# The last batch's second layer: seven products of eighths inside each of seven quarter products

## The chip, the cores and the metric

One core of a Trainium2 chip runs the whole program. The metric is the device time of one execution in microseconds. The core's engines have a queue each and run their own instructions in order: TensorE (PE; its weight loads are listed as PEld), VectorE (DVE), ScalarE (ACT), GpSimd (POOL) and SyncE (SP), which in this kernel issues all DMAs. TensorE writes only into PSUM banks; VectorE or ScalarE must read a bank before it is written anew.

## What is computed

The input x is [4, 2048, 512], f32. Two sublayers follow each other, each with a layer norm in front, a layer norm on its result, and a residual sum:

```python
x = x + _layernorm(_L0_attn_ref(_layernorm(x), w_qkv))       # windowed attention, 16 heads
x = x + _layernorm(_L0_ffn_ref(_layernorm(x), gate..., W1, b1, W2, b2, TW1, Tb1, TW2, Tb2))
```

The second one mixes its weights for each batch b from a base and eight experts, with gates g that are means over the batch's tokens:

```python
mW1 = W1 + jnp.einsum('be,efh->bfh', g, TW1)     # [2048, 512] for each b
mW2 = W2 + jnp.einsum('be,ehf->bhf', g, TW2)     # [512, 2048] for each b
u   = gelu(x @ mW1.T + mb1)                      # first layer
out = u @ mW2.T + mb2                            # second layer
```

## The kernel before, in words

**Stages.** The first half of the time is attention, the second the feed-forward part (from about 1660 us). Under both, a generator, `mixer` (L103), mixes the weights: each step issues the load of an expert's chunk three steps ahead (`load`, L118) and one VectorE instruction (L144). After eight experts of a chunk come four VectorE sums of its quarters (L152 to L155), and one step later the stores to DRAM (`store`, L121 to L132). The steps are written out by hand into the order of the other work: `next(blend)` in attention, `mixing(...)` with a count for each place in the feed-forward part. The DMAs of a step stand in SyncE's queue where the step stands.

**Blocks.** The feed-forward part goes over 16 blocks K of 512 tokens, four to a batch. A block has a first layer of four sets (`begin`, `middle`, `end`), then a second layer (`second`, L1065 on), then the next block follows without a break. `end` of a set (its last product and three pairs of gelus) is put into the next set, and that of the last set into the second layer's first product (`closing`).

**Seven products.** Both layers are done by Winograd's form of Strassen's algorithm: a product of 2x2 quarters by seven products of quarters and sums of quarters. In the second layer a quarter product takes 256 tokens, 1024 hidden units and 256 outputs: `product2` (L1049) runs over 8 chunks of 128 hidden units and 2 token tiles, the tokens' side as the weights of 128x128 and the mixed weights (w2s) as 256 moving columns. Every f32 matmul call leaves two records in the trace. The seven left factors, A11, A12, S1, S2, S4, S3 and A22, lie in DRAM (`m2_d`), 1 MB each; `load_second` (L1042) loads them three products ahead, into three buffers. The right factors are quarters of u and sums of them: t1 and t3 are made by GpSimd in `more_sums` (L1033, L1034); t1 is updated by four GpSimd instructions of 128x512 after product 1 (L1093), and the quarter b21 by four more after product 2 (L1099), each chunk as soon as TensorE has read it. VectorE adds each bank into the block's result y (L1075), and at the end takes the row statistics (`stats`, L87 and L89, GpSimd for the root, L91 and L93). ScalarE normalizes (`standard`, L1165) and VectorE adds the residual (`finish`, L1170), for all blocks but the last one within the next block's sets.

**The next block.** `load_block` (L301) loads the next block's input, fxT, after the second layer's product 0; `right_sums` (L311 to L314) makes four sums over it on VectorE after product 2.

**The last block** does product 6 in two halves by token tile (L1125 on), so that the first tile's rest goes beside the second tile's matmuls; the statistics of a row tile are joined from two halves (`summed`).

**Pools.** The `mix` pool has "exps" (4 buffers), "acc" (2) and "sums" (1). PSUM has eight banks: x and z twice and y once for the first layer, x2, z2 and y2 for the second.

Of the kernel before, what the change touches and what calls it, by code (L numbers as in the profile page):

```python
# [9 lines left out]
F32 = mybir.dt.float32  # L10
# [24 lines left out]
def sandwich(ctx: ExitStack, tc: tile.TileContext, x, w_qkv, gw1, gb1, gw2, gb2, w1, b1, w2, b2, tw1, tb1, tw2, tb2, out):  # L35
# [43 lines left out]
    }  # L79
    m2_d = {b: dram.tile([P, 7, HC, Q], F32, name=f"m2d_{b}") for b in range(NB)}  # L80
    mb2_d = {b: dram.tile([P, D], F32, name=f"mb2d_{b}") for b in range(NB)}
    A11, A12, S1, S2, S4, S3, A22 = range(7)

    def stats(src, tag):
# [16 lines left out]
    def mixer():  # L101
# [19 lines left out]
        def store(b, s, c, acc, sums):  # L121
            rows = acc.rearrange("p h (q d) -> p h q d", d=Q)
            if s == 0:
                early, later = (m1_d[b, c - c % 2, i][:, c % 2] for i in range(2))
                nc.sync.dma_start(early[:, A11 : A12 + 1, :], rows[:, 0])
                nc.sync.dma_start(early[:, S1 : S2 + 1, :], sums[:, 0:2, :])
                nc.sync.dma_start(later[:, S4 - 4, :], sums[:, 2, :])
                nc.sync.dma_start(later[:, S3 - 4 : A22 - 3, :], rows[:, 1])
            else:
                nc.sync.dma_start(m2_d[b][:, A11 : A12 + 1, c, :], rows[:, :, 0, :])  # L130
                nc.sync.dma_start(m2_d[b][:, S1 : S4 + 1, c, :], sums)
                nc.sync.dma_start(m2_d[b][:, S3 : A22 + 1, c, :], rows[:, :, 1, :])  # L132
# [4 lines left out]
        for n, (b, s, c, e) in enumerate(todo):  # L137
# [8 lines left out]
            if e == NX - 1:  # L146
# [9 lines left out]
                late.append(lambda b=b, s=s, c=c, acc=acc, sums=sums: store(b, s, c, acc, sums))  # L156
                yield
        for f in late:
            f()
# [147 lines left out]
    def right_sums(K):  # L307

        b11, b12, b21, b22 = quarters(K)
        t = tT_of[K] = wp.tile([P, 4, 2, Q], F32, tag="w1", name=f"tT_{K}")  # L310
        nc.vector.tensor_tensor(t[:, 0], b12, b11, ALU.subtract)  # L311
        nc.vector.tensor_tensor(t[:, 2], b22, b12, ALU.subtract)
        nc.vector.tensor_tensor(t[:, 1], b22, t[:, 0], ALU.subtract)
        nc.vector.tensor_tensor(t[:, 3], b21, t[:, 1], ALU.subtract)  # L314

# [5 lines left out]
    def hidden(cc, K, pool):  # L321

        if cc in (0, HC):
            t = wp.tile([P, 3, 2, Q], F32, tag="s1" if cc == 0 else "s2", name=f"u{cc}_{K}")
            return t[:, :2].rearrange("p f h t -> p f (h t)")
        return pool.tile([P, 2, TB], F32, tag=f"u{cc}", name=f"u{cc}_{K}")

    us = {}
    blend = mixer()


    with ExitStack() as actx:
# [469 lines left out]
        first[244].append(lambda: load_first(0, 2, 1, wp, "tx"))  # L802
        rest[243].append(lambda: right_sums(0))

# [133 lines left out]
    with ExitStack() as fctx:  # L938
# [90 lines left out]
        def more_sums(K, c):  # L1029

            b12, b22 = us[c][:, :, Q:], us[c + HC][:, :, Q:]
            t1s[c] = wts.tile([P, 2, Q], F32, tag=f"t1_{c}", name=f"t1_{c}_{K}")
            nc.gpsimd.tensor_tensor(t1s[c], b12, us[c][:, :, :Q], ALU.subtract)  # L1033
            nc.gpsimd.tensor_tensor(b12, b22, b12, ALU.subtract)  # L1034
            b, k = divmod(K, NBLK)
            if k == NBLK - 1 and b + 1 < NB:
                for i in range(2):
                    load_first(b + 1, c, i, *home(c, i))

        order = [A11, S1, A12, S2, S4, S3, A22]  # L1040

        def load_second(g):  # L1042

            K, j = divmod(g, 7)
            if K < NBK:
                w2s[g] = wts.tile([P, HC, Q], F32, tag="w2s", bufs=3, name=f"w2s_{g}")
                nc.sync.dma_start(w2s[g], m2_d[K // NBLK][:, order[j]])

        def product2(K, j, bank, right, start, closing=None, tiles=range(2)):  # L1049

            w = w2s[7 * K + j]
            for c in range(HC):
                if c == 2 and closing:
                    end(*closing)
                for t in tiles:
                    nc.tensor.matmul(  # L1056
                        bank[:, t, :],
                        lhsT=right(c - c % 2)[:, c % 2, ts(t, P)],
                        rhs=w[:, c, :],
                        start=(start and c == 0 and t == tiles[0]),  # L1060
                        stop=True,
                        skip_group_check=True,
                    )
            load_second(7 * K + j + 3)

# [3 lines left out]
        def second(K, closing, steps, load_x1):  # L1069
# [47 lines left out]
            Y = bank2("y2", f"py2b_{K}")  # L1117
            if K + 1 < NBK:
                product2(K, 6, Y, b21, True)
                for t in range(2):  # L1120
                    pending.append((K, t + 2, y[1][:, t, :], stats(y[1][:, t, :], f"d{K}_{t + 2}")))
                add(c21, Y, c21)
                steps()
                for t in range(2):
                    pending.append((K, t, y[0][:, t, :], stats(y[0][:, t, :], f"d{K}_{t}")))  # L1125
                yield
                return

            Z = bank2("z2", f"pz2b_{K}")
            product2(K, 6, Y, b21, True, tiles=(0,))  # L1130
            product2(K, 6, Z, b21, True, tiles=(1,))
            for t in range(2):
                standard(K, t + 2, y[1][:, t, :], stats(y[1][:, t, :], f"d{K}_{t + 2}"))
            halves = [small.tile([P, 2, 6], F32, tag="halves", bufs=2, name=f"halves_{t}") for t in range(2)]
            for t in range(2):
                nc.vector.bn_stats(halves[t][:, 0, :], c11[:, t])
            def summed(t, bank):
                nc.vector.tensor_tensor(c21[:, t], bank[:, t, :], c21[:, t], ALU.add)
                nc.vector.bn_stats(halves[t][:, 1, :], c21[:, t])
                mv = small.tile([P, 2], F32, tag="mv", name=f"mv_e{t}")  # L1140
                nc.vector.bn_aggr(mv, halves[t])
                rs = small.tile([P, 1], F32, tag="rs", name=f"rs_e{t}")
                nc.gpsimd.tensor_scalar(rs, mv[:, 1:2], EPS, None, ALU.add)
                nc.gpsimd.tensor_tensor(rs, rs, mhalf, ALU.pow)
                return mv, rs

            sm = summed(0, Y)
            for t in range(2):
                finish(K, t + 2, y[1][:, t, :])
            normalize(y[0][:, 0, :], y[0][:, 0, :], sm)  # L1150
            sm = summed(1, Z)
            finish(K, 0, y[0][:, 0, :])
            normalize(y[0][:, 1, :], y[0][:, 1, :], sm)
            finish(K, 1, y[0][:, 1, :])
            yield

# [66 lines left out]
        nc.sync.dma_start(win[last]["x"], x[NB - 1, L - P :])  # L1223
        for g in range(3):
            load_second(g)
        pending, normed_y = [], []
# [11 lines left out]
        for K in range(NBK):  # L1238
# [5 lines left out]
            for c in range(0, HC, 2):  # L1244
# [32 lines left out]
                for f in hooks.get(("set", n), ()):  # L1277
                    f()
            for j, _ in enumerate(second(K, before, mixing(3, 2, 3, 2, 2, 3, 2), load_x1)):

                if j == (0 if K else 3) and K + 1 < NBK:
                    load_block(K + 1)
                if j == (2 if K else 5) and K + 1 < NBK:
                    right_sums(K + 1)
                for f in hooks.get(("product", K, j), ()):
# [57 lines left out]
```

## Time and profile before

| | |
|---|---|
| median of three runs | 3230.07 us (3229.55 to 3233.14) |
| span of the profiled execution | 3228.7 us |
| TensorE busy | 3211.8 us, 23190 matmul records |
| granted TensorE clock, mean | 0.999 |
| second layer, all 16 blocks (L1056) | 32 records a product, 379 ns each as a record, 6.91 us a product in the chain |
| mixing, VectorE (L144) | 512 instructions of 1361 ns |
| VectorE busy in 2886 to 2934 us (a second layer of the last batch) | 11.57 of 48 us |
| VectorE busy in 2838 to 2886 us (a first layer of the last batch) | 7.93 of 48 us |
| DMA share and rate in 2700 to 2740 us (mixing) | 1.04, 400 GB/s |
| DMA share and rate in 2886 to 2934 us | 0.49, 169 GB/s |

The page gives no other time for the profiled execution than its span; the median of the runs is 1.4 us above it. A record's mean (379 ns) is its time from start to end; records overlap, so the spacing of a stream is the length of a merged stretch by the number of its records. The timeline merges equal instructions that follow each other: start, length, engine, line, operation, output and inputs by name, count, and in brackets the idle time in front and what ended it. The mixing of the last chunk ends at 2778 us; the last batch's blocks (12 to 15) begin at 2835, 2932, 3028 and 3125 us.

### The profile page before, as it was taken

To read this page: it belongs to the slowest core of one execution; us is meant where nothing else is said; L and a number is where in the kernel's file an instruction comes from. 1 tells how busy PE (TensorE), PEld (TensorE's weight loads), DVE (VectorE), ACT (ScalarE), POOL (GpSimd) and SP (SyncE) were. 2 spreads that over 40 slices of the span, in tenths; PEclk is the share of its full clock that TensorE was granted. 3 is DMA by queue.
4 is the path that set the end of the run, shared out by engine and by line. 5 is a ranking of instruction groups with operands and counts; after the bars stand their busy time and mean duration, and the time that the engine had idled before them with its cause. 6 is when DMAs were issued, how large, how long until landed. Compare 5 with 4: busy or idle time off the path is not lost.

```text
span 3228.7 us, 59302 instructions
## 1 busy us (share of the span) xinstructions
PE 3211.8 (99%) x23190; PEld 2690.1 (83%) x23190; DVE 2142.8 (66%) x2995; ACT 1566.3 (49%) x4288; POOL 660.1 (20%) x843
## 2 busy tenths in 40 slices
PE   9999999999999999999999999999999999999999
PEld 7788878788787887878768888888888888888888
DVE  5766666888998889888865665777656776222212
ACT  3777777777777777777761222111222111222111
POOL 0111111111111111110112332333332333231222
PEclk9999999999999999999999999999999999999999
DMA  2111112455555556554687889998889988622332
GB/s 87 50 60 54 41 59 81 131 187 169 196 193 166 177 177 201 192 177 151 220 283 272 317 310 344 352 341 329 318 320 348 355 330 327 238 98 90 131 111 98
DMA packets 316121, 652.02 MB, mean 202 GB/s; under 512 B 22969, under 2 KB 89657, under 8 KB 295490
## 3 DMA queue, kind: packets, MB, share of 16 engines
q1 hardware_dynamic: 315842, 648.22, 57.3%
q8 instruction: 184, 3.01, 0.4%
q14 instruction: 95, 0.78, 0.1%
HBM read 538.03 MB, written 110.10 MB: 201 GB/s over the span
## 4 chain that ended last, share of the span: by engine, by line
PE 96%; DMA 2%; DVE 1%; ACT 1%; issue 0%; POOL 0%; SPq 0%; POOLq 0%; DVEq 0%; ACTq 0%
PE pm L453 23%; PE px L958 13%; PE ptp L621 11%; PE px L1056 10%; PE sc L584 7%; PE pz L958 7%; PE pz L1056 6%; PE po L642 5%; PE py L958 3%; PE py L1056 3%; PE py2b L1056 3%; DMA exps<-in_tw 1%; PE pm L517 1%; PE ptx L287 1%; PE pto L258 1%; PE pt_a L382 1%
## 5 line engine op out<-in xcount | busy, mean ns | idle before, releaser
L144 DVE SCALAR_TENSOR_TENSOR acc<-exps,g,acc 128x1024 f32<-128x1024 f32 x512 | 697.0, 1361 | 75.0 <-DMA exps<-in_tw 69.0
L593 DVE TENSOR_REDUCE nm<-sc 128x2 f32<-128x768 f32 (+1 forms) x512 | 449.3, 918 | 207.7 <-PE sc L584 202.6
L606 ACT ACTIVATE pr<-sc,nm 128x384 f32<-128x384 f32 (+1 forms) x1024 | 572.8, 592 | 10.0 <-DVE nm L593 9.8
L626 ACT COPY prT<-ptp 128x512 f32<-128x512 f32 x732 | 382.9, 595 | 281.4 <-PE ptp L621 281.1
L995 ACT COPY py<-px 128x512 f32<-128x512 f32 x63 | 36.0, 571 | 784.3 <-PE px L958 784.2
L621 PEld LDWEIGHTS ptp<-ident,pr 128*128 128x128 f32 x2944 | 318.1, 141 | 102.3 <-issue 89.8
L621 PE MATMUL ptp<-ident,pr 128*128 128x128 f32 x2944 | 378.9, 278 | 0.0
L958 PE MATMUL px<-tT,w 128*128 128x256 f32 x1512 | 349.6, 379 | 0.6 <-DVE cpv L1018 0.6
L958 PEld LDWEIGHTS px<-tT,w 128*128 128x128 f32 x1512 | 287.2, 190 | 40.0 <-DVE cpv L1018 1.0
L584 PE MATMUL sc<-k,q 32*128 32x384 f32 (+2 forms) x2816 | 243.0, 423 | 3.5 <-ACT pr L606 3.3
L606 ACT ACTIVATION_READ_ACCUMULATOR pr<-sc,nm 128x1 f32 x1024 | 236.5, 231 | 0.0
L1015 DVE TENSOR_TENSOR cpb<-pz,cpb 128x512 f32<-128x512 f32 x63 | 43.4, 690 | 284.7 <-PE pz L958 247.5
L1056 PE MATMUL px<-w2s,u 128*128 128x256 f32 x1024 | 228.9, 379 | 0.7 <-ACT last L292 0.7
L1056 PEld LDWEIGHTS px<-w2s,u 128*128 128x128 f32 x1024 | 194.5, 190 | 27.3 <-ACT last L292 0.9
L91 POOL TENSOR_SCALAR ve_b<-mv_b 128x1 f32<-128x1 f32 x64 | 42.8, 669 | 818.1 <-DVE mv_b L89 818.1
L642 PEld LDWEIGHTS po<-prT,v 128*32 128x32 f32 x5888 | 152.2, 110 | 50.9 <-ACT pr L606 25.4
L642 PE MATMUL po<-prT,v 128*32 128x128 f32 x5888 | 189.7, 275 | 0.2
L584 PEld LDWEIGHTS sc<-k,q 32*128 32x128 f32 x2816 | 118.4, 183 | 74.3 <-issue 53.9
L1033 POOL TENSOR_TENSOR t<-u 128x512 f32<-128x512 f32 x64 | 83.5, 1304 | 464.2 <-ACT u L970 452.2
L453 PE MATMUL pm<-xnT,wqkv 128*128 128x256 f32 x720 | 172.2, 382 | 0.0
L1075 DVE TENSOR_TENSOR y<-px,mb 128x512 f32<-128x512 f32 x48 | 33.1, 690 | 195.8 <-PE px L1056 195.8
L453 PEld LDWEIGHTS pm<-xnT,wqkv 128*128 128x128 f32 x720 | 132.0, 190 | 16.7
(231 smaller groups left out, 5602.2 us busy)
## 6 DMA issues: line engine op xcount, KB each, us to landing
exps<-in_tw SPq DMA_DIRECT2D x512, 512.0 KB, 6.3
w2s<-m2d SPq DMA_DIRECT2D x112, 1024.0 KB, 7.1
acc<-in_w SPq DMA_DIRECT2D x64, 512.0 KB, 6.6
x<-in_x SPq DMA_DIRECT2D x64, 256.0 KB, 4.1
m1d<-acc SPq DMA_DIRECT2D x64, 256.0 KB, 6.8
m2d<-acc SPq DMA_DIRECT2D x64, 256.0 KB, 6.5
w<-m1d SPq DMA_DIRECT2D x16, 1024.0 KB, 8.0
fxT<-xTd SPq DMA_DIRECT2D x16, 1024.0 KB, 8.2
```

Of the source, the lines that this page charges most:

```text
L144: nc.vector.scalar_tensor_tensor(acc, ets.pop(n), g_all[b][:, e : e + 1], acc, ALU.mult, ALU.add)
L453: nc.tensor.matmul(bank[u not in chain][:, half, :], lhsT=a[:, kc, ts(half, P)], rhs=b[:, kc, :], start=(u not in (2, 3, 4) and half == kc ...
L584: nc.tensor.matmul(scs[r // 2][:, r % 2, col : col + nj * W], lhsT=q[rows, g, ts(W_ % WB, W)], rhs=k_of[kb][rows, g, j0 * W : (j0 + nj) * ...
L593: nc.vector.tensor_reduce(st["nm"][:, h : h + 2], scs[u][:, :, : nk * W], AX.X, ALU.max, negate=True)
L606: nc.scalar.activation(pr[:, : nk * W], scs[r // 2][:, r % 2, : nk * W], AF.Exp, bias=st["nm"][:, h : h + 1], accum_out=st["den"][:, h : h ...
L621: nc.tensor.transpose(pt[:, r, :], st["pr"][g * 4 + r][:, ts(j, W)], ident)
L626: nc.scalar.copy(prT, pt)
L642: nc.tensor.matmul(po[r * E : (r + 1) * E, n, :], lhsT=v_of[kb][:, jj, h * E : (h + 1) * E], rhs=prT[:, r, :], start=(j == 0), stop=(j == ...
L958: nc.tensor.matmul(bank[:, f, :], lhsT=factor[:, f, kc * P : (kc + 1) * P], rhs=right[:, kc, :], start=(start and f == 0 and kc == 0), sto ...
L1015: nc.vector.tensor_tensor(S["b"], Z, S["b"], ALU.add)
L1033: nc.gpsimd.tensor_tensor(t1s[c], b12, us[c][:, :, :Q], ALU.subtract)
L1056: nc.tensor.matmul(bank[:, t, :], lhsT=right(c - c % 2)[:, c % 2, ts(t, P)], rhs=w[:, c, :], start=(start and c == 0 and t == tiles[0]), s ...
```

## The change

In the last batch (`DEEP`) each of the seven quarter products of the second layer is itself done by seven products, of eighths: 128 tokens, 512 hidden units and 128 outputs. An eighth product is four matmul calls of 128x128 weights and 128 moving columns; a quarter product has 28 calls in place of 16.

- The left factors lie in another DRAM tensor, `m3_d`, with eight places for each factor: four for its own eighths, four for inner sums. `store` puts the eighths there with six DMAs for each chunk in place of three.
- At the end of `mixer` come 14 more units (7 factors, 2 halves each): two loads of 256 KB, four VectorE sums, two stores of 256 KB. They take the tags "exps" and "acc". They are issued in the second layer of block 11.
- `load_second` loads half a factor at a time, into six buffers; in the last batch four pieces of a factor, 1.84 MB in place of 1 MB. Each of its calls for the last batch also takes one step of the generator.
- The order of the factors in the last batch is A11, S1, A12, S3, S2, S4, A22.
- The inner right sums of each factor's other side are made by `inner_sums`, one product ahead: four VectorE instructions of 128x384 (128x512 for t1), and where the side is a quarter of u, four GpSimd instructions of 128x128 for its first chunk pair.
- `hidden` puts three chunk pairs of u into one tile, `uw0` or `uw1`; t1 is one tile. GpSimd's updates of t1 and of b21 in the last batch are two instructions each, 128x512 and 128x1536.
- `second_deep` reads each bank after each inner product: adds of 128x128 on VectorE, in product 1 copies on ScalarE.
- `right_sums` returns its four instructions; in the last batch they are issued one by one, at the beginnings of products 1, 2, 3 and 6.
- The row statistics of the second half of the columns are issued inside product 6; in the last block, tile 1 of the rest is normalized before the last inner product's result is read.

The core of the diff:

```diff
+            elif b in DEEP:
+                for i, at in enumerate(((0, 7), (3, 6))[c % 2]):
+                    cols = slice(i * P, (i + 1) * P)
+                    nc.sync.dma_start(m3_d[b][:, A11 : A12 + 1, at, c // 2, :], rows[:, :, 0, cols])
+                    nc.sync.dma_start(m3_d[b][:, S1 : S4 + 1, at, c // 2, :], sums[:, :, cols])
+                    nc.sync.dma_start(m3_d[b][:, S3 : A22 + 1, at, c // 2, :], rows[:, :, 1, cols])
...
+        for n in range(len(inner)):
+            if n + 3 < len(inner):
+                load_inner(n + 3)
+            for f in late:
+                f()
+            f11, f21, f12, f22 = (loaded[n][:, i] for i in range(4))
+            res = mix.tile([P, 4, 2, P], F32, tag="acc", name=f"inner_sums_{n}")
+            nc.vector.tensor_tensor(res[:, 0], f21, f22, ALU.add)
+            nc.vector.tensor_tensor(res[:, 1], res[:, 0], f11, ALU.subtract)
+            nc.vector.tensor_tensor(res[:, 2], f11, f21, ALU.subtract)
+            nc.vector.tensor_tensor(res[:, 3], f12, res[:, 1], ALU.subtract)
+            late = [lambda n=n, res=res: store_inner(n, res)]
+            yield
...
+        def load_second():
...
+            if b in DEEP:
+                n = 2 if h < 3 else 1
+                assert next(blend, None) is None
+                t = wts.tile([P, 2, PAIRS2, P], F32, tag="w2s", bufs=6, name=f"w2s_{K}_{j}_{h}")
+                nc.sync.dma_start(t[:, :n], m3_d[b][:, order_deep[j], 2 * h : 2 * h + n])
...
+        def inner_sums(n, low, high):
...
+            return (
+                (t1, t2, t3, t4),
+                ops(nc.vector, high, lambda t: t[:, 1:]),
+                ops(nc.gpsimd, low, lambda t: t[:, 0]),
+            )
...
+        def second_deep(K, closing, load_x1):
...
+            plan = [
+                (c12, bias(0)),
+                (c22, None),
+                (c11, of(c12)),
+                (c21, bias(1)),
+                (c12, of(c12)),
+                (c12, of(c12)),
+                (c21, of(c21)),
+            ]
...
+                if o == 1 and not last_block:
+                    next_block = right_sums(K + 1)
+                if o in (1, 2, 3, 6):
+                    run(next_block, 1)
+                if o == 5:
+                    add(c21, c21, c12)
+                    add(c12, c12, c22)
+                    nc.gpsimd.tensor_tensor(c22, c22, c21, ALU.add)
+
+                inner(0, X, raw(0, 0), True)
+                nc.scalar.copy(Y, X)
+                if o == 0:
+                    end(*closing)
+                inner(1, Z, summed(0), True)
+                emit((1, 1), Z)
+                if o < 6:
+                    prepare(o + 1)
+                    run(pool, 4)
+                if o == 2:
+                    b22 = rights[5]
+                    nc.gpsimd.tensor_tensor(t1[:, 0], b22[0], t1[:, 0], ALU.subtract)
+                    nc.gpsimd.tensor_tensor(t1[:, 1:], b22[1], t1[:, 1:], ALU.subtract)
+                elif o == 3:
+                    for a, s in zip(rights[6], (t1[:, 0], t1[:, 1:])):
+                        nc.gpsimd.tensor_tensor(a, a, s, ALU.subtract)
+                inner(2, X, summed(1))
+                emit((0, 1), X)
+                if o:
+                    run(dve, 1)
+                inner(3, Y, raw(1, 0))
+                emit((0, 0), Y)
+                if o:
+                    run(dve, 1)
+                if o == 6:
+                    row1 = [stats(y[1][:, t, :], f"d{K}_{t + 2}") for t in range(2)]
...
+                inner(4, X, summed(2))
+                add(r[1, 1], X, r[1, 1])
+                run(dve, 1)
+                inner(5, Z, raw(1, 1))
+                add(r[0, 1], Z, r[0, 1])
+                run(dve, 1)
+                if o == 6 and last_block:
+                    sm = half_stats(halves[1], c21[:, 1], 1)
+                    normalize(y[0][:, 1, :], y[0][:, 1, :], sm)
+                inner(6, X, summed(3))
+                emit((1, 0), X)
+                run(dve, 4)
...
+                elif o == 6:
+                    sm = half_stats(halves[0], c21[:, 0], 0)
+                    for t_ in (2, 3):
+                        finish(K, t_, y[1][:, t_ - 2, :])
+                    normalize(y[0][:, 0, :], y[0][:, 0, :], sm)
+                    finish(K, 0, y[0][:, 0, :])
+                    finish(K, 1, y[0][:, 1, :])
```

## The prediction, made before the result was known

> **What bounds the kernel now.** I read the head of the page first, then the share of the chain that ended last, then that chain inside one second layer of the last batch.
>
> ```profile
> span 3228.7 us, 59302 instructions
> ...
> PE 3211.8 (99%) x23190; PEld 2690.1 (83%) x23190; DVE 2142.8 (66%) x2995; ACT 1566.3 (49%) x4288; POOL 660.1 (20%) x843
> ...
> PEclk9999999999999999999999999999999999999999
> ...
> PE 96%; DMA 2%; DVE 1%; ACT 1%; issue 0%; POOL 0%; SPq 0%; POOLq 0%; DVEq 0%; ACTq 0%
> ```
>
> TensorE is busy 3211.8 of 3228.7 us at full granted clock, so only less TensorE work, or a new stall of TensorE, moves the time. The chain in order of time, from 2890 to 2925 us:
>
> ```profile
> 2890.35 6.91 PE pz L1056 x32
> 2897.26 6.91 PE py L1056 x32
> 2904.16 6.91 PE px L1056 x32
> ```
>
> A quarter product is 8 x 2 = 16 matmul calls; each leaves two records (x32), and a product takes 6.907 us, 0.216 us per record of 256 columns, without a gap. The last batch has 4 blocks x 7 = 28 such products, 193.4 us. These, and what stands on the other engines beside them, are what the change touches.
>
> **(a) TensorE work.** A quarter product becomes 7 x 4 = 28 calls of 128 columns, 56 records. What does a 128-column record cost, with its own weight load? The timeline at the start of the span (first TensorE's rows, then those of its weight loads) has four such records of f32 at full clock, and at 1003 us twelve transposes with twelve different weights:
>
> ```profile
> 6.11 0.66 PE L382 MATMUL pt_a<-ident,x 128*128 128x128 f32 x4 [0.69 <-DVE x L98]
> 6.60 0.61 PE L855 MATMUL idle<-ident 128*128 128x128 f32 x4
> ...
> 6.49 0.53 PEld L855 LDWEIGHTS idle<-ident 128*128 128x128 f32 x4
> ...
> 1003.55 1.53 PE L621 MATMUL ptp<-ident,pr 128*128 128x128 f32 x12
> ```
>
> One idle record lasts 0.275, so four in 0.61 start (0.61 - 0.275)/3 = 0.112 apart; the loads (one lasts 0.19) (0.53 - 0.19)/3 = 0.113 apart; the twelve transposes (one lasts 0.278 in the groups) (1.53 - 0.278)/11 = 0.114; from the first transpose to the first idle record it is 0.49/4 = 0.122. Half of a 256-column record would be 0.108. I take 0.111, nearest to the idle rows (0.108 to 0.114): 56 x 0.111 = 6.22 us, so -0.69 us a product (-0.86 to -0.52) and 28 x -0.69 = **-19.3 us** (-24 to -15).
>
> [...]
>
> **(b) Who must read the banks, and when.** An eighth is 8 records, 0.89 us. Within a product, bank X is written by eighths 0, 2, 4, 6, Z by 1 and 5, Y by 3, and each reuse waits for a reader: eighth 4 for the read after 2, eighth 6 for the read after 4, the next product's eighth 1 for the read after 5. All but product 1's copies are 128x128 VectorE adds (estimate 0.28: the 256-column add L1138 takes 0.41, the 512-column L1075 0.69), starting some 0.2 us after the eighth ends. Between them stand VectorE's right-hand sums for the next product, 4 of 128x384 (estimate 0.55, between 0.42 at 256 and 0.69 at 512). Undisturbed, 0.28 + 0.55 fits into 0.89: the read that eighth 6 needs (due at 5.33 us into a product) is done at 4.9. So in products 0, 4 and 5 I charge nothing; product 1's ScalarE copies (L995 takes 0.57 for 512 columns) hide the same way. The slack is 0.4 us, and VectorE is in order, so whatever holds one of its instructions longer stalls TensorE. Four things do.
>
> **(c) VectorE against GpSimd.** The two timelines around 2808 us:
>
> ```profile
> 2807.51 0.69 DVE L1075 TENSOR_TENSOR y<-py,y 128x512 f32<-128x512 f32 x1 [6.22 <-PE py L1056]
> 2808.11 1.35 DVE L311 TENSOR_TENSOR tT<-fxT 128x512 f32<-128x512 f32 x1
> 2809.38 0.68 DVE L312 TENSOR_TENSOR tT<-fxT 128x512 f32<-128x512 f32 x1
> ...
> 2807.64 1.27 POOL L1099 TENSOR_TENSOR u<-u,t 128x512 f32<-128x512 f32 x1 [0.49 <-PE py L1056]
> ```
>
> L311, two inputs in SBUF, takes 1.35 where L312 takes 0.68: it sits until GpSimd's instruction ends at 2808.91, then needs its 0.55. L1075, one input in PSUM, is not held. [...] The change makes two longer ones: the seven-product's own updates of t1 and of the b21 quarter are now issued as 128x512 and 128x1536 (between 1.27 and 3 x 1.27 = 3.80; I take 3.5), and their order puts all four behind each other in products 2 and 3, 2 x (1.27 + 3.5) = 9.5 us of GpSimd, beside 4 small ones for the next right side (0.4 each, between 0.23, the 128x1 L91, and 1.27). VectorE's sums all have two SBUF inputs. By hand, us from the start of product 2, the two engines taking turns: big update 1.8 to 3.1, bigger one 3.1 to 6.6; VectorE's first sum waits from 3.14 to 6.6, then an add; the second sum waits for the next update to 8.3 and ends at 8.75; only then comes the add that eighth 6 needs, 9.05 instead of 4.9. TensorE, due at 5.33, waits 3.7. The third sum waits for the fourth update until 12.25, so the add after eighth 5 ends at 13.0 and the next product's eighth 1 waits another 2.2. **5.9 us in each of 4 blocks: +23.6** (0 if the turns fall well, 8 each = 32 at most, when nearly all of GpSimd's 9.5 is seen).
>
> **(d) The next block's input.** Its load (fxT) is issued when product 0 ends, as before; but the first sum over it, which stood two products later, now stands at the head of VectorE's queue in product 1. In the trace the load is issued 0.37 us behind one of w2s, and the answer on its tile gives the landing:
>
> ```profile
> 2793.69 0.32 SPq L1047 DMA_DIRECT2D w2s<-m2d  x1
> 2794.06 0.42 SPq L301 DMA_DIRECT2D fxT<-xTd  x1
> ...
> DMA to landing us min/median/max: 6.8/6.8/6.8
> ```
>
> After the change the MB ahead of it goes out as two halves, the first 0.9 us earlier: 0.5 + 5.9 = 6.4 us into product 1. Behind it stand the sum (0.68), two right-hand sums (1.0) and the add (0.28): 8.35 against 5.33 due, 3.0 us. **3 blocks: +9.0** (0 to 12).
>
> **(e) Row statistics.** In product 6 two row statistics (L87, L89 twice: 3216.32 to 3218.08, 1.76 us) stand before the add for eighth 6: done at 6.1 instead of 5.33. **3 blocks x 0.8 = +2.4** (0 to 3).
>
> **(f) The end.** The same in the last block, plus two half statistics (0.72): 1.5 us of stall. Then VectorE waits for GpSimd's root of row tile 1 (0.54 + 0.57) before it normalizes it and only then reads the last eighth; add at 9.75, statistics 0.64, two final adds 1.34, normalize 0.55, two final adds 1.33, at 13.6; the output lands 3.1 later as now (3225.63 to 3228.7): 16.7. Now 7.0 us follow TensorE's end, so 6.22 + 7.0 = 13.2 would be even. **+3.5** (0 to 5).
>
> **(g) The weight sums.** 14 units of 512 KB in and 512 KB out stand in block 11's second layer. VectorE needs 4 x 0.42 = 1.7 us each, but the result tile has two buffers, so unit n+2 waits until unit n has landed: 1.7 + 1.6 of issue + some 3.2 of landing (m2d stores: 2.5 to 17.4) per two units of a chain of two, 3.3 us a unit. From about 2820 us the last eleven end near 2854 where TensorE's product 6 ended at 2835; behind them stand statistics and adds, 5.7 us, and block 12's second set can't close its bank before: TensorE, there at 2852, waits until 2860. **+7.4** (0 to 16; the traffic, 14.7 MB, at the 400 GB/s of 2700 to 2740 us takes 37 us, so DMA nearly suffices).
>
> At nothing: w2s in halves (same bytes and buffers, 6 tiles ahead); u and t1 joined into wide tiles (same readers); six stores instead of three per chunk of the last batch, since mixing runs ahead of its use (it ends at 2778, block 12's second layer starts at 2882). If that cover fails, +0 to 5. w2s in the last batch is 1.84 MB a product, 295 GB/s, under the 400 shown.
>
> **Sum** against the span: -19.3 + 23.6 + 9.0 + 2.4 + 3.5 + 7.4 = +26.6, 3255.3; the median of the runs lies 1.4 above the span, so **3257 us**.
>
> **Rivals.** *VectorE keeps up.* If GpSimd's long updates fall into VectorE's waits for banks and each held sum costs under the 0.4 us of slack, and the load lands before 3.3 us, (c), (d) and (g) vanish: -19.3 + 2.4 + 3.5 = -13.4, 3217. For it: VectorE is busy only some 4 of 6.2 us. Against: L311. It decides from 0.4 us on. *Half of it*: GpSimd's updates don't hold the sums (c = 0), the rest stays: +3, 3233, no change. Against it again L311; for it, no row shows a 1536-column instruction. *Worse*: 128-column records with fresh weights take 0.125 (-2.5 us instead of -19.3), or DMA starves at 295 GB/s on top of fxT: 3280. For it: the loads' spacing, 0.113, is as long as the matmuls', so the load may be the bound, and 0.122 was seen at one change of operands.
>
> **Numbers.** The forecast 0.57, with its own range 3240 to 3272; half of it 0.17; keeps up 0.18; worse 0.08. A measurement can tell about 0.2%, 6.5 us, from no change. Slower: 0.57 + 0.08 + 0.03 of half of it = 0.68; same 0.14; faster 0.18. For 8 in 10 the range goes down to the fast rival and up to the worse one: 3217 to 3281.
>
> **What would show it.** In the changed profile: 56 records per product at 0.111 (a); 128x384 sums of 2 to 4 us in products 2 and 3 of each last block, with TensorE idle behind VectorE's adds (c); a sum over fxT released by the DMA in product 1 (d); TensorE idle once near 2852 (g). No idle of TensorE there, or records of 0.125, would make the prediction wrong.

## The result, and the profile after

The changed kernel takes 3277.16 us (median of 4 runs, 3275.59 to 3281.02) against 3230.55 (3229.55 to 3233.14): ratio 1.0145, 95% interval 1.0131 to 1.016. The forecast was 3257, the range 3217 to 3281. The profiled executions differ by 3274.6 - 3228.7 = 45.9 us. The head of the page after, and its share of the chain that ended last:

```profile
span 3274.6 us, 61672 instructions
...
PE 3209.0 (98%) x23862; PEld 2708.4 (83%) x23862; DVE 2274.6 (69%) x3291; ACT 1576.6 (48%) x4332; POOL 707.8 (22%) x911
...
PE 92%; DVE 3%; DMA 3%; ACT 1%; issue 1%; POOL 1%; SPq 0%; POOLq 0%; DVEq 0%; ACTq 0%
```

TensorE is busy for almost as long as before (3211.8) though it has less to do: a record that runs at half the clock counts as busy for its whole length (eight records take 2.07 us at a clock of 0.50 and 1.13 at 1.00). The chain tells more: 8% of it now lies off TensorE, 4% before. The chain in order of time, one undisturbed product of block 12 (seven eighths; "x16" is the last eighth of a product and the first of the next):

```profile
2946.77 1.79 PE px L1295 x16
2948.55 0.89 PE pz L1295 x8
...
2953.02 1.79 PE px L1295 x16
```

From 2946.77 to 2953.02 it is 6.25 us a product, 0.1116 per record. So the change brings 0.65 us a product, 18 us in all, and 64 are lost elsewhere. The timeline of TensorE lists where it sat idle (start, length, work, and in brackets the idle time in front with what ended it); block 12's second set and block 13's second layer:

```profile
2870.02 3.55 PE L1014 MATMUL py<-fxT,w 128*128 128x256 f32 x8 [18.55 <-ACT py L1051]
```
```profile
3025.73 2.07 PE L1295 MATMUL px<-w2s,inner_right 128*128 128x128 f32 x8 [4.78 <-DVE y L1253]
3027.59 0.63 PE L1295 MATMUL px<-w2s,u 128*128 128x128 f32 x2
3028.02 1.49 PE L1295 MATMUL px<-w2s,uw 128*128 128x128 f32 x6
3029.30 1.49 PE L1295 MATMUL pz<-w2s,inner_right 128*128 128x128 f32 x8
3030.63 1.06 PE L1295 MATMUL px<-w2s,inner_right 128*128 128x128 f32 x8
...
3035.83 1.13 PE L1295 MATMUL px<-w2s,inner_right 128*128 128x128 f32 x8 [1.46 <-POOL u L1336]
...
3039.58 1.13 PE L1295 MATMUL pz<-w2s,inner_right 128*128 128x128 f32 x8 [1.73 <-DVE y L1253]
...
3063.47 1.13 PE L1295 MATMUL px<-w2s,inner_right 128*128 128x128 f32 x8 [0.43 <-POOL rs_d L98]
```

After the idle of 4.78 us the next 24 records last from 3025.73 to 3030.63, 4.90 us for what takes 2.68 elsewhere: 2.2 us more that no wait shows. The stretches of the span (length, TensorE's busy time and records, granted clock, DMA share, GB/s) show why: the clock is at 0.50 here. After the two shorter stalls, 1.46 and 1.73, the records run at full rate again (1.13 for eight):

```profile
3024.00:3026.00 2.00, 0.27 (x1) 0.50 0.52 209
3026.00:3028.00 2.00, 2.00 (x10) 0.50 0.01 4
3028.00:3030.00 2.00, 2.00 (x12) 0.50 0.48 111
3030.00:3032.00 2.00, 2.00 (x19) 0.95 0.56 180
```

VectorE's timeline names what it stood at: first the load of the next block's input, then sums beside GpSimd's long instructions (0.55 us when undisturbed):

```profile
3023.65 0.69 DVE L363 TENSOR_TENSOR tT<-fxT 128x512 f32<-128x512 f32 x1 [6.11 <-DMA fxT<-xTd]
...
3031.93 1.86 DVE L1210 TENSOR_TENSOR inner_right<-uw 128x384 f32<-128x384 f32 x1
...
3035.65 3.58 DVE L1210 TENSOR_TENSOR inner_right<-uw 128x384 f32<-128x384 f32 x1
```
```profile
3029.94 3.44 POOL L1333 TENSOR_TENSOR t<-uw,t 128x1536 f32<-128x1536 f32 x1
...
3035.07 3.75 POOL L1336 TENSOR_TENSOR uw<-uw,t 128x1536 f32<-128x1536 f32 x1
```

The table sets all runs side by side. Its stretches come from the starts of TensorE's first record of each layer: block 11's second layer with block 12's first, the second layers of blocks 12, 13 and 14, and block 15's second layer to the end of the span. First layers of blocks 13 to 15 take 46.62 us in every kernel.

| kernel | median, us | ratio, 95% | 11 and 12 | 12 | 13 | 14 | 15, end |
|---|---|---|---|---|---|---|---|
| before | 3230.55 | | 96.69 | 50.08 | 50.07 | 50.07 | 57.07 |
| after | 3277.16 | 1.0145, 1.0131 to 1.016 | 117.61 | 56.19 | 57.14 | 56.26 | 60.66 |
| late_sums | 3261.53 | 1.01, 1.0083 to 1.0117 | 119.20 | 51.57 | 50.99 | 52.91 | 60.63 |
| vector_updates | 3261.61 | 1.0098, 1.0083 to 1.0113 | 119.38 | 54.20 | 52.74 | 52.81 | 56.24 |
| spread_units | 3252.33 | 1.007, 1.0055 to 1.0085 | 98.23 | 57.10 | 55.55 | 55.77 | 60.62 |
| fill_stall | 3279.68 | 1.0151, 1.0136 to 1.0166 | 120.12 | 57.80 | 58.23 | 56.15 | 60.62 |
| later_normalizing | 3273.84 | 1.0135, 1.0121 to 1.0148 | 113.49 | 59.05 | 56.39 | 56.56 | 62.63 |
| units_no_loads | 3264.36 | 1.0104, 1.0091 to 1.0118 | 105.11 | 57.09 | 55.70 | 57.64 | 60.85 |
| all_stalls_out | 3219.74 | 0.9966, 0.9953 to 0.9978 | 97.07 | 46.97 | 46.75 | 46.30 | 54.81 |
| long_updates_back | 3240.56 | 1.0028, 1.0016 to 1.004 | 97.60 | 52.85 | 52.33 | 52.34 | 60.83 |
| updates_in_pieces | 3222.02 | 0.9971, 0.9961 to 0.9981 | 98.30 | 47.94 | 47.35 | 47.35 | 55.97 |
| eased_loads | 3217.6 | 0.9958, 0.9945 to 0.997 | 96.70 | 46.84 | 46.25 | 46.25 | 53.78 |

For the changed kernel the stretches give 20.9 + 6.1 + 7.1 + 6.2 + 3.6 = 43.9 us; the other 2.0 lie ahead of block 11's second layer, which begins at 2784.86 before and 2786.87 after. That is within chance: over the twelve profiled executions, eleven of them of the changed kernel and its variants, it begins between 2782.8 and 2788.5. The one difference found there between these two is the clock at the end of attention (1580 to 1600 us): 0.83 after, 1.00 before, with the same 1.3 us of idle.

### The profile page after: what moved, and what is told of

Read it like the earlier page. It is cut to its first block, busy times and chain, and to the rows that moved or that the text cites. A ratio compares the mean times of both kernels' runs of the same rounds, so it can differ in the third digit from the quotient of the medians.

```text
span 3274.6 us, 61672 instructions
## 1 busy us (share of the span) xinstructions
PE 3209.0 (98%) x23862; PEld 2708.4 (83%) x23862; DVE 2274.6 (69%) x3291; ACT 1576.6 (48%) x4332; POOL 707.8 (22%) x911
## 4 chain that ended last, share of the span: by engine, by line
PE 92%; DVE 3%; DMA 3%; ACT 1%; issue 1%; POOL 1%; SPq 0%; POOLq 0%; DVEq 0%; ACTq 0%
PE pm L509 22%; PE px L1014 13%; PE ptp L677 11%; PE px L1125 7%; PE sc L640 7%; PE pz L1014 6%; PE po L698 5%; PE pz L1125 5%; PE py L1014 3%; PE px L1295 3%; PE py L1125 2%; PE py2b L1125 2%; PE pz L1295 1%; PE pm L573 1%; PE ptx L338 1%; PE pto L309 1%
## 5 line engine op out<-in xcount | busy, mean ns | idle before, releaser
L1014 PE MATMUL py<-fxT,w 128*128 128x256 f32 x504 | 121.0, 384 | 19.4 <-ACT py L1051 19.4
L1125 PE MATMUL px<-w2s,uw 128*128 128x256 f32 x576 | 128.2, 379 | 0.0
L1091 POOL TENSOR_TENSOR t<-uw 128x512 f32<-128x512 f32 x48 | 61.6, 1283 | 299.0 <-ACT uw L1026 299.0
L1065 ACT COPY cpb<-px 128x512 f32<-128x512 f32 x63 | 36.9, 585 | 183.6 <-PE px L1014 183.6
```

The source lines that it names most:

```text
L1014: nc.tensor.matmul(bank[:, f, :], lhsT=factor[:, f, kc * P : (kc + 1) * P], rhs=right[:, kc, :], start=(start and f == 0 and kc == 0), sto ...
L1125: nc.tensor.matmul(bank[:, t, :], lhsT=right(c - c % 2)[:, c % 2, ts(t, P)], rhs=w[:, c % (HC // 2), :], start=(start and c == 0 and t == ...
```

## The experiments

Theory: the gain of (a) is real, and four kinds of stall, each with its own cause, eat it: VectorE's queue of units (g), its wait for fxT (d), its sums held by GpSimd (c), and the clock that halves behind the long ones. Rivals: one common cause (the rate of the DMA), or a clock that falls for another reason.

**late_sums.** The sums over the next block's input are issued later.

```diff
-                if o == 1 and not last_block:
+                if o == 3 and not last_block:
                     next_block = right_sums(K + 1)
-                if o in (1, 2, 3, 6):
+                if o in (3, 4, 5, 6):
```

> The changed kernel with one edit: the four sums over the next block's input (fxT) are issued at the beginnings of products 3, 4, 5 and 6 and no longer of 1, 2, 3 and 6. Theory: in each of blocks 12 to 14 VectorE stood at fxT for some 6 us, TensorE stood idle 4.5 to 5.2 us behind it in product 1, and then ran its next 24 records at half the granted clock, 4.90 us for what takes 2.68. All of it goes: 3 x (4.8 + 0.2 + 2.2) = -21.6 us against the changed kernel's 3277.2, so 3255 to 3258, ratio 1.008 to the kernel before. Rival 1 (only the idle counts, the low clock has another cause): 3 x 5 = -15, 3262. Rival 2 (the load is late for any reader and the sums now hold up products 3 to 6 instead): under -7, 3270 or more.

3261.53, -15.6. That is the size of rival 1, but not for its reason: in product 1 the stall and the half clock behind it are both gone. The mechanism held, the size didn't: TensorE now comes to the next stall earlier and waits longer there. Its stalls behind GpSimd in products 2 and 3 of blocks 12 to 14 grow from 6.1 us (1.55, 3.19, 1.38) to 10.3 (4.19, 2.78, 3.32), and the half clock came back behind two of them; block 13:

```profile
3022.60 2.05 PE L1295 MATMUL px<-w2s,inner_right 128*128 128x128 f32 x8 [2.47 <-POOL u L1336]
```

**vector_updates.** GpSimd's four long updates a block become eight short ones of VectorE, each at a place of its own.

```diff
+            sub = lambda out, x, y: lambda: nc.vector.tensor_tensor(out, x, y, ALU.subtract)
...
+            slots = [(2, 0), (2, 1), (2, 2), (3, 0), (3, 1), (3, 2), (4, 1), (4, 2)]
...
-                if o == 2:
-                    b22 = rights[5]
-                    nc.gpsimd.tensor_tensor(t1[:, 0], b22[0], t1[:, 0], ALU.subtract)
-                    nc.gpsimd.tensor_tensor(t1[:, 1:], b22[1], t1[:, 1:], ALU.subtract)
-                elif o == 3:
-                    for a, s in zip(rights[6], (t1[:, 0], t1[:, 1:])):
-                        nc.gpsimd.tensor_tensor(a, a, s, ALU.subtract)
```

> The changed kernel with one edit: the updates of t1 and of the b21 quarter, four GpSimd instructions of 128x512 and 128x1536 in products 2 and 3, become eight VectorE instructions of 128x512, spread over products 2, 3 and 4 between the reads of the banks. Theory: VectorE's sums were held at a lock by GpSimd's long instructions; TensorE's idle in products 2 and 3 of blocks 12 to 15, 1.9, 3.2, 1.4 and 4.2 us in the trace, 10.7 in all and some 0.2 more per stall, goes: -10 to -12 against 3277.2, so 3265 to 3267, and no 128x384 sum takes over 1 us there. Rival 1 (the prediction's own size, 5.9 a block, part of it hidden in the stall of product 1): -20 or more. Rival 2 (VectorE has no room: 8 x 0.68 = 5.4 us more a block makes it the bound): 0 or slower.

3261.61, -15.5, more than expected: no stall is left in products 2 and 3. The blocks gain 2.0, 4.4, 3.5 and 4.4, 14.3 together. That is more than the 10 to 12 of idle; the clock after the stall of product 1 also came back sooner in blocks 13 and 14 (the eighth after it 1.44 and 1.84 us in place of 2.07). VectorE has room for it: rival 2 is out.

**spread_units.** Nine of the 14 units go into block 12's first layer.

```diff
-                assert next(blend, None) is None
+                assert stored[0] >= min(14, 2 * (j + 1)), (stored[0], K, j, h)
...
+                elif K == 3 * NBLK:
+                    step = mixing(1, 1, 0, 1)
...
-                products2 = second(K, before, mixing(3, 2, 3, 2, 2, 3, 2), load_x1)
+                products2 = second(K, before, mixing(*((3, 2, 3, 1, 1, 0, 0) if K == 3 * NBLK - 1 else (3, 2, 3, 2, 2, 3, 2))), load_x1)
```

> The changed kernel with one edit: of the 14 units of inner weight sums only five are issued in block 11's second layer, the other nine in block 12's first layer, three for every set of seven products instead of up to five for each product of the second layer. Theory: the 18.6 us for which TensorE stands idle at 2851 is VectorE's queue of units, each waiting for the store of the unit two before, ahead of the row statistics for which ScalarE's normalizing, and behind it the copy that TensorE needs, waits. Spread out, the wait of a unit lies beside TensorE's work: -18.6 and -1.7 for the half clock after it, so -18 to -20 against 3277.2, 3257 to 3259. Rival 1 (the rate of the DMA is the bound: 14.7 MB beside 295 GB/s of other traffic): the units stay late and TensorE waits elsewhere, over half of the 20 us remains. Rival 2 (a stall of VectorE in the first layer costs the same wherever it lies): TensorE idles once for each unit, 9 x 2 = 18, no gain.

The stretch of blocks 11 and 12 falls from 117.61 to 98.23, -19.4 as expected; the median falls by 24.8, of which 3.8 lie ahead of that stretch, within the chance named above. The units still end at 2872 and VectorE still waits 17.2 us for their stores, but nothing that TensorE needs soon stands behind them. So it was the place in the queue, not the wait.

**fill_stall.** TensorE is kept busy in the stall of product 1.

```diff
+                if o == 1 and not last_block:
+                    idle = ps_x.tile([P, 2, Q], F32, tag="z", name=f"fill_{K}")[:, 0, :P]
+                    for _ in range(20):
+                        nc.tensor.matmul(idle, lhsT=ident, rhs=ident, start=True, stop=True)
                 inner(6, X, summed(3))
```

> The changed kernel with work added and nothing taken away: in product 1 of blocks 12 to 14, ahead of the eighth that waits (the last), 20 matmul calls of 128x128 on the identity into a bank that nobody reads, 40 records of 0.111 us, 4.5 us. Theory: TensorE's wait for VectorE stays as long, but TensorE is busy in it, so the granted clock stays at 1.00 and the 2.2 us that the 24 records afterwards lost to the half clock come back: 3 x -2.2 = -6.6 against 3277.2, 3270 to 3271; the records after it at 0.111. Rival 1 (the low clock comes from something else, like VectorE's or the DMA's state): no gain, 3277, records at 0.21 again. Rival 2 (the idle isn't filled but lengthened): slower, by up to 3 x 4.5.

3279.68, no gain. The local part of the theory holds: with 4.63 us of other matmuls in the stall, the records behind it run at full rate (eight in 1.16 us, clock 1.00). The 2.2 us are lost again at the next stall, which grew to 2.76 and now brings the half clock in blocks 12 and 13. TensorE's timeline in block 13:

```profile
3022.45 4.63 PE L1367 MATMUL fill<-ident 128*128 128x128 f32 x40
3027.29 1.16 PE L1295 MATMUL px<-w2s,inner_right 128*128 128x128 f32 x8 [0.21 <-DVE y L1253]
...
3036.56 1.13 PE L1295 MATMUL px<-w2s,inner_right 128*128 128x128 f32 x8 [2.76 <-POOL u L1336]
...
3040.31 2.05 PE L1295 MATMUL pz<-w2s,inner_right 128*128 128x128 f32 x8 [1.02 <-DVE y L1253]
```

So the clock followed TensorE's idle time here (0.21 us in front of the eighth and 1.00 in this kernel, 4.78 and 0.50 in the changed one), and rival 1 falls; the expected time failed because stalls in a row aren't independent.

**later_normalizing** and **units_no_loads** take the 18.6 us apart.

```diff
-                for p in pending[:2]:
+                two = 0 if K == 3 * NBLK and c == 0 else 2
+                for p in pending[:two]:
                     standard(*p)
                     normed_y.append(p[:3])
-                del pending[:2]
+                del pending[:two]
```

> The changed kernel with one edit: in block 12 ScalarE's normalizing of the block before starts one set later (sets 1 and 2 in place of 0 and 1). Theory: at 2851 TensorE stood behind ScalarE's copy of Y, the copy behind the normalizing, and that behind the row statistics that stand last in VectorE's queue of units. With the normalizing gone from its front, the copy runs at once, TensorE goes on for two products (3.5 us) and then waits for VectorE's two adds (done at 2867.8 in the changed kernel): TensorE's idle at this place falls from 18.6 us to 12 to 13, -4 to -6.5 us, 3271 to 3273. Rival 1 (the copy waits for something else, as for the bank): 18 to 20 us remain. Rival 2 (only ScalarE is in the way, VectorE isn't): the idle falls under 5 us.

```diff
             if n + 3 < len(inner):
-                load_inner(n + 3)
+                loaded[n + 3] = loaded[n]
```

> The changed kernel with work left out: units 3 to 13 of the inner weight sums load nothing and compute from the tiles of units 0 to 2, so the last batch's second layer uses wrong factors; their VectorE work and stores stay. That takes away 5.8 MB of DMA in 2805 to 2860 and nothing of the chain of two result buffers. Theory: a unit takes 4.0 us in place of the 3.3 that I had worked out because the stores land slower (4.8 us in the middle, 2.2 at the fastest) at a DMA share of 0.9 to 1.0; without the loads they land in 2.5 to 3.5 us, the 14 units end some 10 to 15 us earlier and TensorE's idle at 2851 falls from 18.6 to 4 to 10 us. Rival (the chain of the two buffers with its issue times on SyncE and VectorE's other work sets the pace, not the rate): landing may fall, but the last unit still ends after 2857 and over 14 us of idle remain.

With the normalizing out of its way TensorE goes on to 2855 and then waits 13.0 us for VectorE; without the units' loads it waits 5.4. The rows of the two kernels, and the landing of the units' stores with (first) and without (second) the loads:

```profile
2868.42 3.78 PE L1014 MATMUL px<-tT,w 128*128 128x256 f32 x8 [13.03 <-DVE cpv L1074]
```
```profile
2855.59 3.78 PE L1014 MATMUL py<-fxT,w 128*128 128x256 f32 x8 [5.40 <-ACT py L1051]
```
```profile
DMA to landing us min/median/max: 2.2/4.8/6.3
```
```profile
DMA to landing us min/median/max: 2.2/2.7/6.3
```

The last unit ends at 2862.4 in the changed kernel and 2848.0 without loads: the DMA's load sets the pace of the chain of two result buffers. In the changed kernel VectorE waits for the stores of earlier units and never for a unit's own loads. A landing 2.1 us shorter on a chain of two is some 1.05 us a unit, an estimate of 13.7 of the 14.4 us; what the loads' own issues on SyncE cost wasn't tried. The times are 3273.84 (-3.3, under the expected 4 to 6.5) and 3264.36 (-12.8). With the normalizing moved, the stretch gains 4.1 and block 12's second layer loses 2.9 again.

**all_stalls_out.** The edits of late_sums, vector_updates and spread_units together, and another edit of which these are the main lines:

```diff
                 emit((1, 1), Z)
+                if o == 6:
+                    row_stats(0)
...
                 if o == 6:
-                    row1 = [stats(y[1][:, t, :], f"d{K}_{t + 2}") for t in range(2)]
+                    row_stats(1)
...
-                    normalize(y[0][:, 1, :], y[0][:, 1, :], sm)
+                    standard(K, 1, y[0][:, 1, :], sm)
```

> The changed kernel with the three edits of late_sums, vector_updates and spread_units together, and the row statistics of the last product moved: one row tile's after its second eighth and one after its fourth, the half statistics of the last block into product 4, and in the last block one normalizing on ScalarE in place of VectorE and one residual sum a product earlier. Theory: what the change gains by 128-column records, 0.65 us for each of 28 products, is real, and the stalls were all that hid it. A second layer is then 7 x 6.25 + 1.73 + 0.3 = 45.8 us instead of 50.07: -4.3 in blocks 12 to 14; the last block -4.6 and at its end between -1 and +1; block 11's second layer +1.5 as in spread_units. Sum -16 (-13 to -18): 3214, between 3212 and 3218, ratio 0.995, which is the first rival of the prediction, reached by four edits. Rival 1 (with the known stalls gone new ones appear, as in fill_stall, where the wait moved to the next product): 3225 to 3235. Rival 2 (the clock drops for other reasons than the stalls): granted clock under 0.995 and over 3220.

3219.74, ratio 0.9966 (0.9953 to 0.9978): faster than the kernel before by a third of a per cent, 1.7 us above the expected range. The blocks gain 3.1 to 3.8 in place of 4.3: two pauses over 0.2 us are left in them (0.35 in block 12, 0.26 in block 13, which ends with a load of w2s), and a second layer with neither takes 46.25, as eased_loads shows, not 45.8. No stall over 1 us is left, and the page shows TensorE's lesser work now:

```profile
PE 3195.1 (99%) x23862; PEld 2694.8 (84%) x23862; DVE 2274.9 (71%) x3322; ACT 1579.6 (49%) x4333; POOL 673.7 (21%) x896
```

**long_updates_back, updates_in_pieces, eased_loads** start from all_stalls_out. The first puts the old GpSimd updates back (the minus lines of vector_updates). The others:

```diff
-            sub = lambda out, x, y: lambda: nc.vector.tensor_tensor(out, x, y, ALU.subtract)
+            sub = lambda out, x, y: lambda: nc.gpsimd.tensor_tensor(out, x, y, ALU.subtract)
```
```diff
-                if j == (0 if K else 3) and K + 1 < NBK:
+                if b in DEEP:
+                    if j < 2 and K + 1 < NBK:
+                        load_part(K + 1, j)
+                elif j == (0 if K else 3) and K + 1 < NBK:
                     load_block(K + 1)
...
-                if o == 4:
+                if o == (2 if last_block else 4):
                     load_x1(K, 2)
                     load_x1(K, 3)
```

> The kernel of all_stalls_out with one part undone: the updates of t1 and b21 are GpSimd's again, two instructions of 128x512 and two of 128x1536 a block in products 2 and 3. It prices the prediction's term (c) with no other stall beside it (predicted: 5.9 us a block). Theory: VectorE's sums are held at GpSimd's instructions as in late_sums: TensorE idles 2.5 us in product 2 and 0.3 to 1.9 after it, and where the first of these halves the granted clock up to 2 us follow: 3 to 6 us a block, +12 to +24 against all_stalls_out's 3219.7, 3232 to 3244. Rival 1 (VectorE has room for waiting once its other work is moved away): under +5. Rival 2 (the prediction's 5.9 in every block): +24 or more.

> The kernel of all_stalls_out with one word changed: the same eight updates of 128x512 at the same eight places are GpSimd's in place of VectorE's. GpSimd's time on them is as much as in long_updates_back, 8 x 1.27 = 10.2 us a block, but no instruction is longer than 1.27. Theory (a sum of VectorE is held until GpSimd's running instruction ends): a sum now waits at most 1.27 and lasts at most 1.8 us, in a product with two updates the reads run some 1 us over the slack of 0.4: 0.3 to 1 us for each of three products, +1 to +3 a block, +4 to +12 against all_stalls_out, 3224 to 3232, and no halved clock, since no stall reaches 2 us. Rival 1 (what counts is GpSimd's total time, not the length of one instruction): as long_updates_back, +12 or more. Rival 2 (VectorE doesn't feel updates of 128x512 at all): within 2 of all_stalls_out.

> The kernel of all_stalls_out with loads moved: the next block's input (fxT) in two halves, one after product 0 and one after product 1, in place of 1 MB at once, and the last block's loads of its residual rows after products 2 and 3 in place of 4. In all_stalls_out blocks 12 to 14 still lose some 1 us each in pauses of 0.2 to 0.4 us ahead of eighths whose weights (w2s) land late behind fxT, and the last block 0.9 in product 6. Theory: the pauses go, -0.5 to -1 in each of four blocks, 3216 to 3218, ratio 0.995 to 0.996. Rival (the pauses come from VectorE or from SyncE's order, not from the load ahead): within 1 of 3219.7.

long_updates_back: +20.8, and in the stretches 5.9, 5.6, 6.0 and 6.0 us a block in the profiled execution. Each block has the same two stalls there, the second at half clock; block 12:

```profile
2908.14 1.13 PE L1310 MATMUL px<-w2s,inner_right 128*128 128x128 f32 x8 [2.46 <-POOL u L1353]
2911.89 2.05 PE L1310 MATMUL pz<-w2s,inner_right 128*128 128x128 f32 x8 [0.93 <-DVE y L1257]
```

That execution took longest of the five, 3245.64 at a mean granted clock of 0.994. Two others took 3235.69 and 3236.03 at 0.998, 4.0 us a block above all_stalls_out: by the clock, most of the half clock is missing there.

updates_in_pieces: 3222.02, under the expected 3224 to 3232 and 2.3 above all_stalls_out, and 0.6 to 1.2 a block in the stretches. The same work of GpSimd in pieces costs a sixth of what it costs in long instructions, or a quarter of the 4.0. By the medians it can't be told from no cost, but the hold is there; VectorE's timeline in block 13 (its 128x384 sum takes 0.55 alone):

```profile
2996.55 1.66 DVE L1214 TENSOR_TENSOR inner_right<-uw,inner_right 128x384 f32<-128x384 f32 x1
```

eased_loads: 3217.6, the fastest kernel here, 0.42% under the kernel before (0.3 to 0.55%). The pause for w2s in block 13 is gone, the one of 0.35 in block 12 isn't, and the last block gains 1.0; against all_stalls_out the intervals overlap.

One common cause, the rate of the DMA, is out: vector_updates moves the same bytes and takes 14.3 us off the blocks. The rate counts in (g), and by the landing of fxT it may count in (d).

## Why the prediction was right in sign, and 20 us short

3277.16 lies in the range of 3217 to 3281, but above the forecast's own 3240 to 3272. The range reached so far up for the rival "Worse", neither of whose conditions came: the records take 0.1116 and not 0.125, and no wait names starved weights (w2s). That it held the result is in part luck. That rival's "-2.5 us" should read +2.6 (56 x 0.125 = 7.0 against 6.907, 28 times); its 3280 has the right sign.

- **(a), (b) right.** 6.25 us a product in place of the forecast 6.22, -18 in place of -19.3. A weight load with every record (23862 of each on the page) costs little: 0.1116 us is 3% over half of a 256-column record (0.108). In undisturbed products the reads of the banks hide.
- **(g) is the step that failed.** "block 12's second set can't close its bank before: TensorE, there at 2852, waits until 2860." It stopped at 2851.5 and waited until 2870.0. The mechanism was right, the sizes weren't: a unit took 3.9 us (14 from 2810.1 to 2860.9) and not 3.3 because the stores landed in 4.8 and not 3.2, so the last one ended at 2862.4 and not 2854 (units_no_loads: landing 2.7, idle 5.4); ScalarE's copy for TensorE stood behind the normalizing that waited for the statistics behind the units, 2 us and two products that could have gone ahead (later_normalizing); and the first product afterwards ran at half clock, 1.7 more. The stretch lost 20.9 where +7.4 was forecast: 13.5 of the 19.3 us by which the sum was short.
- **(d) right in place, short in size.** Forecast 3.0 a block. The load landed 7.3 to 8.0 us after its issue (5.9 estimated), TensorE idled 4.5 to 5.2, and then worked 4.5 to 6.2 us at the half clock, which cost 2.2 to 3.1. With the 1.7 in (g) that is 9.3 us over the four places, for which the prediction had no term at all.
- **(c) right in mechanism, its size met by luck.** The forecast 5.9 a block is what long_updates_back measures in its profiled execution when nothing else stalls (5.6 to 6.0), but by other parts: 2.5 + 0.9 to 1.1 of idle, not 3.7 + 2.2, and the rest by the half clock; its two shortest executions come to 4.0. In the changed kernel it was 4.2 of idle in the last block and 1.4 to 3.2 in blocks 12 to 14: less there, probably because GpSimd worked on while TensorE stood in product 1. That a sum is held until GpSimd's instruction ends had been seen beside one of 1.27 us only; the changed kernel shows it beside a long one (a sum of 3.58 us beside 3.75, 0.55 undisturbed).
- **(e) 0.43 in place of 0.8; (f) right.** TensorE's last record ends 8.8 us before the end of the span in place of 6.8, and product 6 of the last block stalls for 0.9: +3 where +3.5 was forecast. The edits costed at nothing cost the changed kernel nothing that shows: no wait of TensorE in it names w2s. With other stalls away w2s does come late, by 0.26 us in all_stalls_out and 0.86 once in vector_updates.
- **Rivals.** "VectorE keeps up", 3217, didn't happen. With the stalls removed by hand the change gives 3219.7 and 3217.6; that its sum came so near is in part luck, since it kept 5.9 us for (e) and (f), which those kernels mostly moved away. What it said of VectorE's room was right, what it said of the order of its queue was not.

Blocks 12 to 14 lost 19.4 (14.6 forecast), the last block 3.6 (4.6), the stretch ahead 2.0 (0): 13.5 + 4.8 - 1.0 + 2.0 = 19.3, the miss.

## What to carry to other kernels

When work is taken from the bounding engine by giving more small pieces to another, ask for every instruction of that other engine's queue what it may wait for (a load, a store's landing, a third engine's long instruction) and what stands behind it; most of the cost here went with three orderings, not with any lack of time. Stalls in a row are not a sum: one hides part of the next, so price a stall by removing all the others and putting it back alone. And count a long stall of TensorE (here 2.46 us and more) with the half clock that may follow it (here it cost 2.2 to 3.1 us behind stalls of 4.5 to 5.2).

## What the runs showed of the hardware that was not expected

The granted clock fell to 0.50 during an idle stretch of TensorE and stayed there when TensorE worked again: for 6.8 us in block 13 of the changed kernel (3023.4 to 3030.2, TensorE busy again from 3025.73), for 3.4 us in block 13 of late_sums. In the last batch of the profiled runs every idle stretch of 4.35 us or more had slow records behind it. Of 16 stretches between 2.46 and 2.77 us, 11 had the half clock within the next 5 us and 5 not, with the same instructions around them; none under 2 us brought it by itself (behind the longest of these, 1.98 us in block 12 of spread_units, eight records took 1.13).

In the changed kernel's last batch the clock fell at 2856.13, 2920.98, 3023.38 and 3129.20 and rose again 17.07, 6.83, 6.83 and 6.83 us later, all of them multiples of 3.413 us apart (from 3023.38 to 3030.21 and on to 3129.20: 2 and 29 times). Rows of this length set TensorE's busy time (second figure) beside the clock (behind the count). The first two are block 13 of late_sums, the others block 15 of spread_units:

```profile
3018.77:3022.18 3.41, 1.36 (x13) 1.00 0.93 332
3022.18:3025.59 3.41, 2.99 (x14) 0.50 0.34 132
```
```profile
3210.05:3213.47 3.42, 1.51 (x13) 1.00 0.61 173
3213.47:3216.88 3.41, 1.69 (x15) 1.00 0.55 159
```

With 2.05 us of idle in the first of two rows the second ran at half clock, with 1.91 it didn't. Cut the same way, the changed kernel's last batch has four rows at full clock with 2.25 us of idle or more while TensorE still has work to come (2.25, 2.43, 3.41 and 3.42): each has one at half clock behind it, and none of the rows with 1.73 or less has. Behind a row at half clock came full clock where TensorE was idle in it for 0.24 us or not at all, and half clock again at 0.67 and more. That it goes by the idle time in such a row is the author's reading of these rows; no run was made to test it. By it a stretch of 2.5 us halves the clock or doesn't by where it falls: the 2.46 us in block 15 of the changed kernel lie as 1.15 and 1.31 in two rows, and the clock stays at 1.00. The figure isn't the same for all work: at the end of attention the changed kernel has 0.96 us of idle in a row (1586.37 to 1589.78) and the half clock behind it, and in eight of the twelve executions the mean clock from 1560 to 1700 us is 0.98 or 0.99. Why is open.
